# One bias column, one shared PSUM bank, VectorE's additions and three places in a schedule: a four-layer image kernel on one core

## The chip, the cores and the metric

The kernel runs on one core of a Trainium2 chip. Its time is device microseconds from the first to the last instruction, the median of several runs. The core has five engines that run beside each other: TensorE (PE, matmuls, with weight loads as PEld), VectorE (DVE), ScalarE (ACT), GpSimd (POOL) and SyncE (SP, which issues DMAs). Matmul results land in PSUM, in banks of 2 KB per partition; everything else lives in SBUF. Each engine executes its instructions in the order in which the program lists them, and waits on semaphores for the others.

## What is computed

The input x has 4 samples of 256 channels and 48 x 48 = 2304 positions, all in float32. Four layers follow, each of the form x = x + f(groupnorm(x)):

```python
def _gn(v, G=32, eps=1e-5):              # normalise over groups of 8 channels
    g = v.reshape(B_, G, C_ // G, H_, W_)
    m = jnp.mean(g, axis=(2, 3, 4), keepdims=True)
    s = jnp.var(g, axis=(2, 3, 4), keepdims=True)
    return ((g - m) / jnp.sqrt(s + eps)).reshape(v.shape)

# layer 0: attention with 8 heads of 64 channels over 2304 positions
qkv = jnp.einsum('oc,bchw->bohw', w_qkv, x)
q, k = _l2norm_last(q), _l2norm_last(k)          # over the positions
sim = jnp.einsum('bhdi,bhdj->bhij', q, k) * 10.0
out = jnp.einsum('bhij,bhdj->bhid', jax.nn.softmax(sim, axis=-1), v)
y0 = jnp.einsum('oc,bchw->bohw', w_out, out) + b_out

# layer 1: a gate from a depthwise convolution on a 16 x 16 grid
x_tem = _blur_pool(_max_pool_3x3(x), stride=3)   # 48 x 48 -> 16 x 16
s = x_h1 + x_w1 + x_h2 + x_w2                    # four depthwise strips of 11 x 3 taps
y1 = x * upsample(sigmoid(batchnorm(s)))

# layer 2: attention with one head of 64 channels, then a projection and a batch norm
f = jnp.einsum('bnc,bcm->bnm', theta_x, phi_x) * c1 ** (-0.5)
y2 = batchnorm(W @ (softmax(f) @ g_x))

# layer 3: a channel gate, a 3 x 3 depthwise convolution, an instance norm
y3 = leaky_relu(instancenorm(dwconv3x3(x * a)))
```

## The kernel before

The attentions are cut into blocks of 384 query positions (a "unit"). A unit takes its 2304 key positions in 18 blocks of 128, two to a group, so nine groups (NG = 9). For every group, TensorE makes the scores of this group and weighs the values of the last one; between the two it does what other jobs are placed in that group. ScalarE turns scores into exponentials (`pt`), eight buffers of which exist. The sums of the exponentials are added up in `acc` outside TensorE:

```python
PAIRED = (1, 3, 5, 7)

def scores(u, j):
    ps = sc_tile()                     # 2 buffers of 2 banks
    ...  # 4 matmuls, each on a quadrant of the array
    pt = ppool.tile([P, 2, SL], F32, tag="pt", name="pt")
    nc.scalar.activation(pt, ps[:, :, :SL], AF.Exp, scale=u["scale"])      # L277

def add_up(u, g):
    pts = [u["pt"][j] for j in range(g * G, (g + 1) * G)]
    terms = u.setdefault("terms", [])
    if g in u["paired"]:               # GpSimd adds the two blocks first
        half = hpool.tile([P, 2, SL], F32, tag="half", name="half")
        nc.gpsimd.tensor_add(half, pts[0], pts[1])                         # L302
        pts = [half]
        ready, u["terms"] = terms, pts
    else:
        ready, u["terms"] = terms + pts, []
    ...
    for term in ready:
        nc.vector.tensor_add(u["acc"], u["acc"], term)                     # L317
```

The main loop gives each group its order, and ScalarE's part of layer 1 (a product of a 16 x 16 image and one tap's weight, 761 ns each) in portions by the place of the group in its unit:

```python
QUOTA = (2, 1, 0, 1, 2, 1, 2, 1, 2)    # taps after group 0, 1, ... of a unit
AT_TOTAL, AT_FOLD, AT_INVERT, AT_DIVIDE, AT_AFTER = 3, 2, 5, 9, 11

for t, (u, g, st) in enumerate(groups):
    for j in range(g * G, (g + 1) * G):
        scores(u, j)
    do(fills, t, lambda rank: rank < 1)
    if prev is not None:
        add_up(*prev)
    do(due, t)
    ...
    do(fills, t)                       # jobs on TensorE, in the order of their rank
    ...                                # jobs of layer 1
    if prev is not None:
        ...  # weigh(pu, j) for the two blocks of the last group
        if pg == NG - 1:
            last(pu, t)                # ScalarE copies the result out of PSUM (raw)
    take_taps(QUOTA[clock["slot"]])
```

Beside one pair of heads, the projections of the next pair are made, one chunk of 384 columns per unit, in the unit's third group. All of these jobs, the output projection and the products of the group norms share two PSUM buffers, the `pj` tiles of one bank each:

```python
def pj_tile():
    return ps_pj.tile([P, 512], F32, tag="pj", name="pj")   # 2 buffers

# inside gn(): sums over the 8 channels of a group, by a product with gmat
def squares():
    ps = pj_tile()
    nc.tensor.matmul(ps[:, 0:NK], lhsT=gmat, rhs=mv[:, :, 0], start=True, stop=True)   # L197
    nc.vector.tensor_copy(gm, ps[:, 0:NK])
    ...
def inverse():
    ps = pj_tile()
    nc.tensor.matmul(ps[:, 0:NK], lhsT=gmat, rhs=res["sq"], start=True, stop=True)     # L207
    ...
# "placed" norms: both as jobs of rank 3.5 in a unit's third group, one unit apart

def out_bias():                        # one per pair of heads, in the third group of its second unit
    ps = pj_tile()
    for k in range(NK):
        nc.tensor.matmul(ps[:, k : k + 1], lhsT=wo[:, p, k * P : (k + 1) * P],
                         rhs=at["bias_v"], start=True, stop=True)                      # L550
    ...  # VectorE copies it to pair["bo"]

# a chunk: rank 1 q, rank 2 values, rank 3 k (each: products into a pj tile, ScalarE copies out)
# out_proj part(k): rank 2.5 (0 for sample 0) and rank 4
def part(k):
    ps = pj_tile()
    nc.tensor.matmul(ps[:, :SL], lhsT=wo[:, p, k * P : (k + 1) * P], rhs=o["o"], ...)  # L649
    nc.vector.scalar_tensor_tensor(                                                    # L654
        xs, ps[:, :SL], pair["bo"][:, k : k + 1], xs, ALU.add, ALU.add)
```

In layer 2 the projections of the next sample (L1009, L1030) have fixed places among the 27 groups of a sample, and so have the statistics of the output, which VectorE takes from PSUM (L1057, L1065):

```python
AT_PLACE = 6
if b > 0:
    spread(work, stats(b - 1, 1), [4, 5])
    spread(work, stats(b - 1, 2), [13, 14])
if b + 1 < B:
    spread(work, stats(b, 0), [22, 23])
    ...
    if b + 2 < B:
        for c in range(L2C):
            work[NG * c + AT_PLACE] = slices[c] + slices[c + L2C]
else:
    spread(work, stats(b, 0), [14, 15])
    spread(work, stats(b, 1), [23, 24])
```

Layer 0 of samples 1 to 3 runs beside layer 1 of the sample before it; layer 1 of the last sample runs beside layer 2.

Of the kernel before, what the change touches and what calls it, by code (L numbers as in the profile page):

```python
# [14 lines left out]
P = 128  # L15
HW = 48
N = HW * HW
NK = 2
# [56 lines left out]
def usual_path(  # L75
# [96 lines left out]


    GN_TICKS = NSL + 4

    def gn(b, res, halves=range(NK), slices=range(NSL), first=False, placed=False):

        if "st" not in res:
            res["st"] = small.tile([P, NK, NSL, 6], F32, tag="gn_st", name="gn_st")
        st = res["st"]  # L180
        if first:
            for s in slices:
                for k in halves:
                    nc.vector.bn_stats(st[:, k, s, :], X[b][:, k, s * SL : (s + 1) * SL])
        for s in () if first else slices:
            for k in halves:
                nc.vector.bn_stats(st[:, k, s, :], X[b][:, k, s * SL : (s + 1) * SL])
            if s % 2 or len(halves) == NK:
                yield 0
        mv = small.tile([P, NK, 2], F32, tag="gn_mv", name="gn_mv")  # L190
        for k in range(NK):
            nc.vector.bn_aggr(mv[:, k, :], st[:, k].rearrange("p s f -> p (s f)"))
        gm = small.tile([P, NK], F32, tag="gn_gm", name="gn_gm")

        def squares():
            ps = pj_tile()
            nc.tensor.matmul(ps[:, 0:NK], lhsT=gmat, rhs=mv[:, :, 0], start=True, stop=True)  # L197
            nc.vector.tensor_copy(gm, ps[:, 0:NK])
            dev = small.tile([P, NK], F32, tag="gn_dev", name="gn_dev")
            nc.vector.tensor_sub(dev, mv[:, :, 0], gm)  # L200
            res["sq"] = sq = small.tile([P, NK], F32, tag="gn_sq", name="gn_sq")
            nc.vector.tensor_mul(sq, dev, dev)
            nc.vector.tensor_add(sq, sq, mv[:, :, 1])

        def inverse():
            ps = pj_tile()
            nc.tensor.matmul(ps[:, 0:NK], lhsT=gmat, rhs=res["sq"], start=True, stop=True)  # L207
            gv = small.tile([P, NK], F32, tag="gn_gv", name="gn_gv")
            nc.vector.tensor_scalar(gv, ps[:, 0:NK], GN_EPS, None, ALU.add)
            res["rs_"] = small.tile([P, NK], F32, tag="gn_rs", name="gn_rs", bufs=6)  # L210
            rsqrt(res["rs_"], gv)

        def done():
            rs = res["rs_"]
            nm = small.tile([P, NK], F32, tag="gn_nm", name="gn_nm", bufs=6)
            nc.vector.tensor_scalar(nm, gm, -1.0, None, ALU.mult)
            nb = small.tile([P, NK], F32, tag="gn_nb", name="gn_nb", bufs=6)
            nc.vector.tensor_mul(nb, nm, rs)
            res["rs"], res["nb"], res["nm"] = rs, nb, nm

        if placed:

            t = clock["t"] + 1
            t += (AT_AFTER - t) % NG
            fills.setdefault(t, []).append((3.5, squares))
            fills.setdefault(t + NG, []).append((3.5, inverse))
            due.setdefault(t + NG + 3, []).append(done)
            yield 1
            return
        yield 3  # L230
        squares()
        yield 2
        inverse()
        yield 2
        done()
        yield 1
# [82 lines left out]
    def total(u):  # L319

        ab = [pj_tile()[:, :SL] for _ in range(2)]
        for h, c in enumerate(HALVES):
            for r, out in zip(HALVES, ab):
                nc.tensor.matmul(
                    out[c], lhsT=ones[r], rhs=u["acc"][r, h, :], start=True, stop=True
                )
        if "shift" in u["of"]:
            rows = [op.tile([P, SL], F32, tag="o", name="row") for _ in ab]
        else:
            row = hpool.tile([P, 2, SL], F32, tag="half", name="row")  # L330
            rows = [row[:, i, :] for i in range(2)]
        for i in range(2):
            nc.scalar.copy(rows[i], ab[i])
        u["l6"] = small.tile([P, 2, LW], F32, tag="l6", name="l6")
        for c in HALVES:
            for i in range(2):
                nc.sync.dma_start(
                    u["l6"][c, i, :],
                    rows[i][c.start : c.start + 1, :].rearrange("o (p w) -> o p w", w=LW),
                )  # L340
# [49 lines left out]
        nc.vector.tensor_add(lsum[:, 0:1], lsum[:, 0:1], two[:, 0:1])  # L390
        nc.vector.tensor_tensor(lmin[:, 0:1], lmin[:, 0:1], two[:, 1:2], ALU.min)

    due, fills, clock = {}, {}, {}

    taps_due = []

    QUOTA = (2, 1, 0, 1, 2, 1, 2, 1, 2)

    def take_taps(n):
        for _, fn in taps_due[:n]:  # L400
# [98 lines left out]
    def project(b, norm, pair):  # L499
# [18 lines left out]
        def norms():  # L518

            w = at["w"]  # L520
            ps = pj_tile()
            for k in range(NK):
                nc.tensor.matmul(
                    ps[:, 0:1], lhsT=w[:, k, 2, :], rhs=norm["nb"][:, k : k + 1],
                    start=k == 0, stop=k == NK - 1,
                )
            at["bias_v"] = small.tile([P, 1], F32, tag="bias_v", name="bias_v", bufs=3)
            nc.vector.tensor_copy(at["bias_v"], ps[:, 0:1])
            for k in range(NK):
                nc.scalar.activation(  # L530
                    w[:, k], w[:, k], AF.Identity, scale=norm["rs"][:, k : k + 1]
                )
# [11 lines left out]
                fetch(0)  # L544
                fetch(1)

        def out_bias():
            ps = pj_tile()
            for k in range(NK):
                nc.tensor.matmul(  # L550
                    ps[:, k : k + 1], lhsT=wo[:, p, k * P : (k + 1) * P],
                    rhs=at["bias_v"], start=True, stop=True,
                )
            bo = small.tile([P, NK], F32, tag="bo", name="bo", bufs=3)
            if p == 0:
                nc.vector.tensor_add(bo, ps[:, 0:NK], vec[:, V_BOUT, :])
            else:
                nc.vector.tensor_copy(bo, ps[:, 0:NK])
            pair["bo"] = bo

        def qk(s, t):
            cols = slice(s * SL, (s + 1) * SL)
            to = pair["qk"[t]][:, cols]
            n = SL + (s == 0 and not direct)
            ps = pj_tile()
            for k in range(NK):
                nc.tensor.matmul(  # L567
                    ps[:, :n], lhsT=at["w"][:, k, t, :], rhs=xs[s][:, k, :n],
                    start=k == 0, stop=k == NK - 1,
                )  # L570
            if s == 0 and direct:
                for k in range(NK):
                    nc.tensor.matmul(
                        ps[:, SL : SL + 1], lhsT=at["w"][:, k, t, :],
                        rhs=norm["nm"][:, k : k + 1], start=k == 0, stop=k == NK - 1,
                    )
            if s == 0:
                nc.scalar.copy(at["bias"][:, t : t + 1], ps[:, SL : SL + 1])
            if direct and t:

                nc.vector.tensor_scalar(to, ps[:, :SL], at["bias"][:, t : t + 1], None, ALU.add)
            else:
                nc.scalar.activation(to, ps[:, :SL], AF.Identity, bias=at["bias"][:, t : t + 1])
# [41 lines left out]
        def rescale(c0, c1):  # L625
# [7 lines left out]
            nc.vector.tensor_scalar(q, q, at["sc"], None, ALU.mult)  # L633

        return {
            "prefetch": prefetch, "norms": norms, "start": start, "out_bias": out_bias,
            "chunk": chunk, "qk": qk, "squares": squares, "values": values,
            "scale": [
                scale, lambda: rescale(0, 1), lambda: rescale(1, 3), lambda: rescale(3, 6)
# [3 lines left out]
    def out_proj(b, p, c, pair, o):  # L643
# [2 lines left out]

        def part(k):
            ps = pj_tile()
            nc.tensor.matmul(  # L649
                ps[:, :SL], lhsT=wo[:, p, k * P : (k + 1) * P], rhs=o["o"], start=True,  # L650
                stop=True,
            )
            xs = X[b][:, k, cols]
            nc.vector.scalar_tensor_tensor(  # L654
                xs, ps[:, :SL], pair["bo"][:, k : k + 1], xs, ALU.add, ALU.add
            )
# [3 lines left out]
    def l0_unit(b, p, c, pair):  # L660
        hold = {}

        def o_tile():
            hold["o"] = op.tile([P, SL], F32, tag="o", name="o")
            return hold["o"]

        return {
            "pt": {}, "qc": slice(c * SL, (c + 1) * SL), "paired": PAIRED,
            "soon": b == B - 1 and p == NPAIR - 1 and c == NCH - 1,
            "scale": 1.0, "of": pair, "o": o_tile,  # L670
            "after": out_proj(b, p, c, pair, hold),
# [182 lines left out]

    TAPS_AT_ONCE = 12

    AT_PLACE = 6

    def strips_pe(b, k, norm, res):

# [366 lines left out]
    for i, (b, p) in enumerate(order):  # L1227
        work, others = {}, []
        if i + 1 < len(order):
            new = projs[i + 1]  # L1230
            work[0] = [new["start"]]
            for s in range(NCH):
                work[NG * s + AT_CHUNK] = new["chunk"](s)
            work[NG + AT_CHUNK].append(new["out_bias"])
            for slot, fn in zip((n - 5, n - 3, n - 2, n - 1), new["scale"]):
                work[slot] = [fn]
            if i + 2 < len(order):
# [25 lines left out]
    for b in range(B):  # L1263
# [19 lines left out]
            if b + 2 == B:  # L1283
                others.append((follow(start, slices, norms2[b + 1]), 1000, 0, n))
        else:
            spread(work, stats(b, 0), [14, 15])
            spread(work, stats(b, 1), [23, 24])
            others.append((diagonals(), NK * len(PE_TAPS), 4, 22))
        phases.append(([l2_unit(b, c, twos[b]) for c in range(L2C)], work, others))
# [12 lines left out]
        fn()  # L1302
    for s in range(NCH):
        projs[0]["values"](s)
    projs[0]["out_bias"]()
    projs[1]["norms"]()
    attend(phases)
    for k in range(NK):
# [1278 lines left out]
```

## Time and profile before

| | |
|---|---|
| time, median of 3 runs | 3639.22 us (3636.34 to 3643.51) |
| span of the profiled run | 3637.4 us |
| mean granted TensorE clock | 0.985 |
| DMA | 95.69 MB, mean 26 GB/s |

In the profile, a line such as L649 is a line of the kernel. `pj<-o,wo` says that a tile `pj` is written from `o` and `wo`. A group of instructions has its count, the union of its busy times, the mean duration of one, and after the bar the idle time of its engine just before it, with what ended that idle time. An fp32 matmul leaves two records. In the table of waits, the columns are the total in us, the number of times and the longest.

### The profile page before, as it was taken

To read this page: it belongs to the slowest core of one execution; us is meant where nothing else is said; L and a number is where in the kernel's file an instruction comes from. 1 tells how busy PE (TensorE), PEld (TensorE's weight loads), DVE (VectorE), ACT (ScalarE), POOL (GpSimd) and SP (SyncE) were. 2 spreads that over 40 slices of the span, in tenths; PEclk is the share of its full clock that TensorE was granted. 3 is DMA by queue.
4 is the path that set the end of the run, shared out by engine and by line. 5 is a ranking of instruction groups with operands and counts; after the bars stand their busy time and mean duration, and the time that the engine had idled before them with its cause. 6 is when DMAs were issued, how large, how long until landed. Compare 5 with 4: busy or idle time off the path is not lost. (4 is left out here: it accounts for less than half of the span.)

```text
span 3637.4 us, 88927 instructions
## 1 busy us (share of the span) xinstructions
PE 3488.9 (96%) x37490; PEld 1762.7 (48%) x37490; DVE 2600.2 (71%) x3268; ACT 2423.3 (67%) x3889; POOL 1387.0 (38%) x886
## 2 busy tenths in 40 slices
PE   8999999999999999999999999999999998999786
PEld 4555555554444444544444445444444445654332
DVE  3555555577889787778797877777977778575678
ACT  4665666666875886668858866688588655554476
POOL 2333333333333333333333333333333356573333
PEclk9999999999999999999999999999999999999798
DMA  2211111111111111211111111111111100000001
GB/s 91 47 26 21 26 22 27 22 25 22 24 23 24 20 27 22 72 26 24 22 25 22 26 20 26 22 25 22 25 17 26 18 5 7 8 6 6 27 32 76
DMA packets 115433, 95.69 MB, mean 26 GB/s; under 512 B 56544, under 2 KB 110416, under 8 KB 114256
## 3 DMA queue, kind: packets, MB, share of 16 engines
q1 hardware_dynamic: 112128, 87.73, 13.2%
q8 instruction: 296, 4.85, 0.5%
q10 hardware_dynamic: 2896, 2.18, 0.2%
q14 instruction: 113, 0.93, 0.1%
HBM read 56.98 MB, written 11.80 MB: 19 GB/s over the span
## 5 line engine op out<-in xcount | busy, mean ns | idle before, releaser
L277 ACT ACTIVATE pt<-sc 128x768 f32<-128x768 f32 x1944 | 1475.5, 811 | 770.5 <-PE sc L271 762.0
L302 POOL TENSOR_TENSOR half<-pt 128x768 f32<-128x768 f32 x477 | 948.1, 1989 | 1604.0 <-ACT pt L277 1500.0
L271 PE MATMUL sc<-q,k 64*64 64x384 f32 x13824 | 1273.5, 483 | 5.1 <-ACT pt L277 5.1
L291 PE MATMUL av<-pt,v 64*64 64x384 f32 x13824 | 1276.8, 484 | 0.0
L317 DVE TENSOR_TENSOR acc<-acc,pt 128x768 f32<-128x768 f32 x792 | 958.7, 1210 | 80.9 <-DVE acc L317 1.8
L271 PEld LDWEIGHTS sc<-q,k 64*64 64x64 f32 x13824 | 521.5, 133 | 607.5 <-issue 536.5
L291 PEld LDWEIGHTS av<-pt,v 64*64 64x64 f32 x13824 | 519.1, 133 | 591.9 <-issue 559.3
L317 DVE TENSOR_TENSOR acc<-acc,half 128x768 f32<-128x768 f32 x459 | 476.6, 1038 | 300.9 <-POOL half L302 299.7
L654 DVE SCALAR_TENSOR_TENSOR x<-pj,bo,x 128x384 f32<-128x384 f32 x192 | 118.4, 617 | 438.6 <-PE pj L649 438.0
L827 ACT ACTIVATE prod<-pd,wt 128x256 f32<-128x256 f32 x486 | 336.1, 761 | 0.2
L567 PE MATMUL pj<-xs,w 128*128 128x384 f32 (+1 forms) x720 | 275.3, 505 | 1.7 <-POOL xs L511 0.9
L372 POOL TENSOR_TENSOR o<-o,rinv 128x384 f32<-128x384 f32 x95 | 117.0, 1232 | 362.9 <-DMA rinv<-rinv 330.9
L567 PEld LDWEIGHTS pj<-xs,w 128*128 128x128 f32 x720 | 124.1, 189 | 129.8 <-issue 35.9
L291 PE MATMUL av<-pt,qv 64*64 64x384 f32 x1728 | 178.3, 506 | 0.0
L649 PE MATMUL pj<-o,wo 128*128 128x384 f32 x384 | 161.9, 506 | 15.4 <-DVE x L654 8.1
L271 PE MATMUL sc<-qv,kd 64*64 64x384 f32 x1728 | 170.8, 489 | 2.4 <-ACT pt L277 2.4
L850 DVE TENSOR_REDUCE prod<-prod 128x256 f32<-128x1280 f32 x114 | 168.5, 1478 | 4.5 <-ACT prod L827 4.5
L311 DVE TENSOR_TENSOR acc<-pt 128x768 f32<-128x768 f32 x99 | 150.6, 1521 | 10.8 <-ACT pt L277 10.8
L1541 PE MATMUL one<-pad,diag 64*64 64x384 f32 x1536 | 136.6, 501 | 19.0 <-ACT pad L1511 11.8
L598 PEld LDWEIGHTS pj<-w,xs 128*128 128x128 f32 x1080 | 134.5, 191 | 24.1
L598 PE MATMUL pj<-w,xs 128*128 128x128 f32 x1080 | 134.9, 275 | 0.0
L368 POOL TENSOR_TENSOR o<-raw 128x384 f32<-128x384 f32 x95 | 117.6, 1238 | 0.0
(242 smaller groups left out, 2584.5 us busy)
## 6 DMA issues: line engine op xcount, KB each, us to landing
xs<-in_x_dram SPq DMA_DIRECT2D x90, 384.0 KB
rinv<-rinv SPq DMA_DIRECT2D x208, 94.5 KB
out_dram<-x SPq DMA_DIRECT2D x18, 384.0 KB
l<-row SPq DMA_DIRECT2D x416, 1.5 KB
w<-in_wqkv_dram SPq DMA_DIRECT2D x32, 192.0 KB
x<-in_x_dram SPq DMA_DIRECT2D x4, 1152.0 KB
x<-in_x_dram SPq DMA_DIRECT2D x9, 384.0 KB
rinv<-ls SPq DMA_DIRECT2D x208, 1.5 KB
```

What stands on the lines that cost most here:

```text
L271: nc.tensor.matmul(ps[c * D : (c + 1) * D, h, :SL], lhsT=u["of"]["k"][r, j0 : j0 + D], rhs=u["of"]["q"][r, u["qc"]], start=True, stop=True,)
L277: nc.scalar.activation(pt, ps[:, :, :SL], AF.Exp, scale=u["scale"])
L291: nc.tensor.matmul(u["av"][h * D : (h + 1) * D, half, :SL], lhsT=value(u, j, h)[r], rhs=pt[r, h, :], start=j == 0, stop=j == JB - 1,)
L302: nc.gpsimd.tensor_add(half, pts[0], pts[1])
L311: nc.vector.tensor_add(u["acc"], ready[0], ready[1])
L317: nc.vector.tensor_add(u["acc"], u["acc"], term)
L567: nc.tensor.matmul(ps[:, :n], lhsT=at["w"][:, k, t, :], rhs=xs[s][:, k, :n], start=k == 0, stop=k == NK - 1,)
L598: nc.tensor.matmul(ps[:, i * P : (i + 1) * P], lhsT=xs[s][:, k, i * P : (i + 1) * P], rhs=at["w"][:, k, 2, :], start=k == 0, stop=k == NK - 1,
L649: nc.tensor.matmul(ps[:, :SL], lhsT=wo[:, p, k * P : (k + 1) * P], rhs=o["o"], start=True, stop=True,)
L827: nc.scalar.activation(bufs[n % 3][:, :, min(n, 1) + i].rearrange("p (r c) -> p r c", c=AS), pd[:, PAD + dr : PAD + dr + AS, PAD + dc : PA ...
L850: nc.vector.tensor_reduce(to, bufs[n % 3][:, :, : min(n, 1) + len(taps)], AX.X, ALU.add)
L1541: nc.tensor.matmul(self.ps[s][h][HALVES[h ^ e], :SL].rearrange("p (r c) -> p r c", c=HW), lhsT=diag[self.k][r, 2 * n + e, :], rhs=self.win ...
```

## The change

It has five parts. The bias of the output projection no longer has matmuls of its own: it is written into a 385th column of the tile that the output projection multiplies anyway, once per pair of heads. The products of the group norms go into two unused columns of the PSUM bank that k's products have just been written to, so that they do not take a `pj` tile of their own. In layer 0 of samples 1 to 3, which runs beside layer 1, VectorE adds all 18 blocks itself, and GpSimd none. The portions of taps change for two places of a unit. In layer 2, the places of the projections are one group later, and two statistics steps of the last sample two groups later. The purpose is to take work and waits off TensorE.

```diff
+        def columns():
+            if of_k.get("t") == clock["t"]:
+                return of_k["ps"][:, 448 : 448 + NK]
+            return pj_tile()
+
         def squares():
-            ps = pj_tile()
+            ps = columns()
 ...
         def inverse():
-            ps = pj_tile()
+            ps = columns()
 ...
-    QUOTA = (2, 1, 0, 1, 2, 1, 2, 1, 2)
+    QUOTA = (1, 1, 0, 2, 2, 1, 2, 1, 2)
 ...
-        def out_bias():
-            ps = pj_tile()
-            for k in range(NK):
-                nc.tensor.matmul(
-                    ps[:, k : k + 1], lhsT=wo[:, p, k * P : (k + 1) * P],
-                    rhs=at["bias_v"], start=True, stop=True,
-                )
-            ...
 ...
             ps = pj_tile()                       # qk(s, t): t = 1 is k
+            if t:
+                of_k["ps"], of_k["t"] = ps, clock["t"]
 ...
         def part(k):
             ps = pj_tile()
+            n = SL + (c == 0)
             nc.tensor.matmul(
-                ps[:, :SL], lhsT=wo[:, p, k * P : (k + 1) * P], rhs=o["o"], start=True,
+                ps[:, :n], lhsT=wo[:, p, k * P : (k + 1) * P], rhs=o["o"][:, :n], start=True,
                 stop=True,
             )
+            if c == 0:
+                if k == 0:
+                    pair["bo"] = small.tile([P, NK], F32, tag="bo", name="bo", bufs=3)
+                bo = pair["bo"][:, k : k + 1]
+                if p == 0:
+                    nc.vector.tensor_add(bo, ps[:, SL:n], vec[:, V_BOUT, k : k + 1])
+                else:
+                    nc.vector.tensor_copy(bo, ps[:, SL:n])
 ...
         def o_tile():
-            hold["o"] = op.tile([P, SL], F32, tag="o", name="o")
-            return hold["o"]
+            hold["o"] = op.tile([P, SL + 1], F32, tag="o", name="o")
+            if c == 0:
+                nc.gpsimd.tensor_copy(hold["o"][:, SL:], pair["bias_v"])
+            return hold["o"][:, :SL]
 ...
-            "pt": {}, "qc": slice(c * SL, (c + 1) * SL), "paired": PAIRED,
+            "pt": {}, "qc": slice(c * SL, (c + 1) * SL), "paired": () if b else PAIRED,
 ...
-    AT_PLACE = 6
+    AT_PLACE = 7
 ...
-            work[NG + AT_CHUNK].append(new["out_bias"])
 ...
-            spread(work, stats(b, 0), [14, 15])
+            spread(work, stats(b, 0), [16, 17])
```

More of the change, by code (lines that the diff above doesn't have):

```diff
@@ L174, in usual_path @@
     GN_TICKS = NSL + 4
+    of_k, clock = {}, {"t": -1}
     def gn(b, res, halves=range(NK), slices=range(NSL), first=False, placed=False):
@@ L327, in total @@
         if "shift" in u["of"]:
-            rows = [op.tile([P, SL], F32, tag="o", name="row") for _ in ab]
+            rows = [op.tile([P, SL + 1], F32, tag="o", name="row")[:, :SL] for _ in ab]
         else:
@@ L391, in note @@
         nc.vector.tensor_tensor(lmin[:, 0:1], lmin[:, 0:1], two[:, 1:2], ALU.min)
-    due, fills, clock = {}, {}, {}
+    due, fills = {}, {}
     taps_due = []
-    QUOTA = (2, 1, 0, 1, 2, 1, 2, 1, 2)
+    QUOTA = (1, 1, 0, 2, 2, 1, 2, 1, 2)
     def take_taps(n):
@@ L526, in norms @@
                 )
-            at["bias_v"] = small.tile([P, 1], F32, tag="bias_v", name="bias_v", bufs=3)
-            nc.vector.tensor_copy(at["bias_v"], ps[:, 0:1])
+            pair["bias_v"] = small.tile([P, 1], F32, tag="bias_v", name="bias_v", bufs=3)
+            nc.vector.tensor_copy(pair["bias_v"], ps[:, 0:1])
             for k in range(NK):
@@ L545, in start @@
                 fetch(1)
-        def out_bias():
-            ps = pj_tile()
-            for k in range(NK):
-                nc.tensor.matmul(
-                    ps[:, k : k + 1], lhsT=wo[:, p, k * P : (k + 1) * P],
-                    rhs=at["bias_v"], start=True, stop=True,
-                )
[L554 to L559, printed above, removed]
         def qk(s, t):
@@ L635, in project @@
         return {
-            "prefetch": prefetch, "norms": norms, "start": start, "out_bias": out_bias,
+            "prefetch": prefetch, "norms": norms, "start": start,
             "chunk": chunk, "qk": qk, "squares": squares, "values": values,
@@ L1304, in usual_path @@
         projs[0]["values"](s)
-    projs[0]["out_bias"]()
     projs[1]["norms"]()
```

## The prediction

> **What bounds the kernel now.** I read the views in this order: busy time of the engines, stretches of the span, TensorE's waits, then the timeline around each kind of wait. First line 1 of the page:
>
> ```profile
> PE 3488.9 (96%) x37490; PEld 1762.7 (48%) x37490; DVE 2600.2 (71%) x3268; ACT 2423.3 (67%) x3889; POOL 1387.0 (38%) x886
> ```
>
> TensorE is busy 96% of the span. The table of stretches (us, then busy PE, PEld, DVE, ACT, POOL, granted clock, DMA) says where it is not:
>
> ```profile
> 750.00:2930.00 2180.00, 2153.06 (x23070) 1060.01 (x23066) 1709.68 (x1986) 1576.30 (x2535) 788.12 (x466) 1.00 0.15 25
> 2930.00:3445.00 515.00, 460.91 (x5070) 262.96 (x5066) 358.30 (x449) 264.56 (x416) 286.03 (x182) 0.93 0.07 10
> 40.00:750.00 710.00, 708.77 (x7678) 360.50 (x7680) 365.61 (x502) 431.85 (x688) 241.20 (x182) 1.00 0.15 29
> ```
>
> From 40 to 750 us (sample 0's attention) TensorE never rests. From 750 to 2930 (attention of samples 1 to 3 beside layer 1) 27 us are idle, in layer 2 (2930 to 3445) 54. So the only things that can move the time are instructions TensorE need not issue and waits that hold it. A page's busy time hides short waits, because a matmul's end is modelled. I therefore took start-to-start times: a block of eight quadrant matmuls (16 records) starts 1.29 us after the last when nothing holds it. By that measure TensorE loses about 4 us up to 750, 56 us from 750 to 2930 and about 60 in layer 2 and its end. Of the 56, some 22 (waits of about 0.1 us for evictions between q, v and k) are not touched by the change. The larger waits, from TensorE's table (total, times, longest):
>
> ```profile
> PE pj L649 <- DVE x L654: 8.1, 7, 1.8
> PE pj L1057 <- DVE bst L1065: 7.7, 5, 4.2
> PE sc L271 <- ACT pt L277: 7.5, 31, 2.4
> PE pj L1009 <- DVE bst L1065: 6.8, 3, 4.0
> PE pj L197 <- DVE x L654: 2.9, 3, 1.0
> PE pj L1030 <- DVE bias L984: 2.5, 1, 2.5
> ```
>
> Every one of them names an engine that is not full but late at one moment. The page's groups show why VectorE is late:
>
> ```profile
> L302 POOL TENSOR_TENSOR half<-pt 128x768 f32<-128x768 f32 x477 | 948.1, 1989 | 1604.0 <-ACT pt L277 1500.0
> L317 DVE TENSOR_TENSOR acc<-acc,pt 128x768 f32<-128x768 f32 x792 | 958.7, 1210 | 80.9 <-DVE acc L317 1.8
> ```
>
> The mean of 1210 ns mixes two kinds. Single records between 750 and 2930 take 958 ns where GpSimd is idle and up to 2.56 us where it runs.
>
> **What the Trainium skill says.** "SBUF — State Buffer", Who interferes with whom: a VectorE instruction with two SBUF inputs and a GpSimd instruction that reads SBUF exclude each other for a whole instruction. The trace agrees: 958 ns alone, 1.6 to 2.6 us beside a GpSimd add. Summing what VectorE's records last over the undisturbed duration of their own kind in 750 to 2930 gives 317 us, of which 269 overlap the pair adds of L302. "PSUM — Partial Sum Buffer", PSUM bank collisions: two engines must not touch one bank and quadrant at once, so a matmul into a bank that ScalarE is reading has to be held by a semaphore even if the columns differ. Nothing in the kernel before shows this; it decides part two below. "TensorE: Matmul & The Clock Gate", What's actually happening: idle TensorE is put on half clock for windows of about 3.4 us. The trace agrees: half-clock stretches of 3.4 or 6.8 us begin at 1164, 2772, 3089, 3236 and 3353 us, each right after a wait of 1.9 to 4.3 us. A long wait so costs half such a stretch more, 1.7 or 3.4 us.
>
> **Part 1, the bias column.** Four one-column matmul records (an fp32 matmul leaves two) leave each head pair, with their weight loads:
>
> ```profile
> 980.11 0.81 PE L649 MATMUL pj<-o,wo 128*128 128x384 f32 x2
> 980.95 0.61 PE L550 MATMUL pj<-bias_v,wo 128*128 128x1 f32 x4
> 981.48 1.52 PE L291 MATMUL av<-pt,v 64*64 64x384 f32 x16
> ```
>
> From the last projection to the next block are 1.37 us. Without the bias it would be 0.325 between the two passes + 0.415 to the next block = 0.74. So 0.63 us x 15 pairs = 9.4 us, all on TensorE's path. The 385th column costs 32 x 1/384 of 0.65 us, nothing. The bias takes 32 VectorE instructions of about 0.16 us in place of 16, and 16 more on GpSimd, all beside other work. Sum -9.
>
> **Part 2, the norms' products in k's bank.** Nine normalisations run inside the attention, two products each: 18. Here is one before (886.30 is k's product):
>
> ```profile
> 886.30 1.56 PE L567 MATMUL pj<-xs,w 128*128 128x384 f32 x4
> 887.69 0.28 PE L207 MATMUL pj<-gn_sq,gmat 128*128 128x2 f32 x2
> 887.89 0.58 ACT L583 ACTIVATE k<-pj,bias 128x384 f32<-128x384 f32 x1 [1.65 <-PE pj L567]
> 888.22 0.91 PE L649 MATMUL pj<-o,wo 128*128 128x384 f32 x2 [0.25 <-DVE gn_gv L209]
> ```
>
> Before, the product goes to the other bank and the projection after it waits 0.25 us for VectorE to read it. In the changed program the product carries a wait on ScalarE instead, that is on k's eviction, which ends at 888.47. It would then start near 888.52 rather than 887.69, and the projection near 888.85 rather than 888.22: 0.6 us later. Fifteen such, +9 us; the other three now wait 1.1 us for a late VectorE (line L197 of the waits) and would get 0.6 shorter, -2. Sum +7. This part should cost time.
>
> **Part 3, VectorE adds alone.** 72 blocks (samples 1 to 3, four pairs, six chunks). Per block before: one add at 1664 ns, eight at 1281, four at 993 = 15.9 us. After: 17 at about 0.958 = 16.3, plus what the two remaining GpSimd instructions per block (1.3 and 1.2 us) disturb. In sum 288 more adds x 0.958 = 276 us against 269 us of exclusion that goes: VectorE's busy time hardly changes. What changes is lateness: it no longer waits for `half` (106 us of idle time in that stretch) and no add lasts 2.5 us. At 1163 the projection waited 1.76 us behind two adds of 2.63, one of 2.56 and a maximum of 2.22 us. Without the pair add these come to about 2 us less. So most of the 8.4 us (start to start) behind L654, and the one wait at L984 (2.6 us, behind adds of 4.14 for two and 1.74), should go: -7 and -2. The half clock after the waits at 1163 and 2772 goes with them, 1.7 + 3.4 us: I count -4.
>
> **Part 4, the taps' quota.** Waits of `sc` on `pt` come once per block where taps run, 29 times, always in the group after a block's end, where ScalarE has the copy of `raw` and two taps. They show as 0.17 us, but start to start it is 1.64 instead of 1.29:
>
> ```profile
> 972.12 1.47 PE L291 MATMUL av<-pt,v 64*64 64x384 f32 x16
> 973.76 1.56 PE L271 MATMUL sc<-q,k 64*64 64x384 f32 x16 [0.17 <-ACT pt L277]
> ```
>
> One tap (0.5 us of ScalarE's issue) moves to the fourth group, where ScalarE idles 0.29 us before its next exponential. 29 x 0.345 = 10 us; I count -9.5.
>
> **Part 5, layer 2's places.** The three waits of L1009 (1.4, 4.1 and 1.5 us) come where the projections follow a statistics step of the group before; a group later VectorE has 2.6 us more: -5.5. At 3348.16 two statistics steps fall in one group and TensorE waits 4.3 us; in the change they are three groups apart: -4. Less half clock behind these, some 3 us. Sum -12.5.
>
> **Sum.** -9 + 7 - 13 - 9.5 - 12.5 = -37. Something unforeseen usually takes some of it back, so I take -33: 3606 us, 0.9% less.
>
> **Rivals.** (a) VectorE becomes the late engine. Per block of about 30 us beside the taps it has 16.3 us of adds, about 6 of reductions, 2 to 3 of the rest, and it must keep up group by group (1.92 of 2.58 us, and 1.48 more where a reduction falls). For it: the reductions sat in groups that had no add, and these have two now. Against: eight `pt` buffers and the long third group (7 us) absorb 2 to 3 us. If TensorE waited 0.5 us per block more, +36 us: 3640. (b) The bank of k: if ScalarE is later than in the sample shown, every norm's product costs 1 us, +9 more: 3615. (c) The waits removed are hidden behind others at once (the next group's `pj` waits for the same late VectorE). Then only parts 1 and 4 pay, against part 2: -12, about 3627. (d) Half clock: a stretch of 37.5 us at 3403 lies in the turn to layer 3, and costs up to 19 us; if the turn shifts it may shorten or lengthen, 5 to 10 us either way.
>
> **Range and chances.** (c) and (b) give the upper side, all parts in full with luck in the clock the lower: 3588 to 3630. Faster by over 2% would need 73 us, more than all named waits; slower by over 2% would need (a) twice over.
>
> **What would show it.** No L550 row; `sc <- ACT pt` down to a few; a new row of the norms' product waiting for ACT `k`, 18 times about 0.6 us idle; L302 at 189 instead of 477; L317 between 750 and 2930 at a mean near 1.0 us; `L649 <- x` and `L984` near zero; the rows with `bst` below 5 us together. I am wrong if VectorE's rows grow in TensorE's waits, or if the stretch from 750 to 2930 does not shrink by 15 us or more.

## The result and the profile after

The changed kernel takes 3605.97 us (median of 4 runs, 3603.77 to 3606.74) against 3639.8 us before (median of 4 runs, one more than in the table of the time before): ratio 0.9906, 95% interval 0.9889 to 0.9923, some 34 us less. In the changed kernel the lines have moved: L197 and L207 (the norms' products) are L204 and L214, L271 (scores) L278, L302 (pair adds) L309, L317 (adds) L324, L511 (a two-column copy on GpSimd that the projections read) L518, L649 and L654 (output projection and its addition) L645 and L658, L894 (layer 1's products) L901, L973 (a product for the bias of layer 2's projections) L980, L984 (that bias) L991, L1009 and L1030 (the projections) L1016 and L1037, L1057 and L1065 (statistics) L1064 and L1072.

The page's first part, and then the table of stretches over the same two windows as before:

```profile
PE 3469.3 (96%) x37426; PEld 1754.9 (49%) x37426; DVE 2607.0 (72%) x3572; ACT 2411.9 (67%) x3889; POOL 824.1 (23%) x614
```

```profile
750.00:2930.00 2180.00, 2163.09 (x23316) 1066.38 (x23310) 1746.58 (x2319) 1579.30 (x2556) 238.29 (x200) 1.00 0.15 25
2930.00:3445.00 515.00, 464.07 (x5150) 265.42 (x5146) 356.71 (x480) 274.48 (x439) 283.54 (x180) 0.94 0.06 10
```

TensorE's share is still 96%. In the first window its idle time fell from 27 to 17 us; in the second it hardly moved, from 54 to 51. GpSimd's busy time fell by 40%, and VectorE's busy time stayed at 2607 us, though it has 304 more instructions.

TensorE's waits (total, times, longest):

```profile
...
PE pj L901 <- DVE bst L1072: 6.7, 3, 4.1
...
PE pj L214 <- ACT k L578: 5.8, 8, 0.9
PE pj L204 <- ACT k L578: 5.4, 8, 0.7
...
PE pj L1064 <- DVE bst L1072: 5.1, 6, 1.0
...
PE sc L278 <- ACT pt L284: 2.9, 2, 2.4
...
PE pj L645 <- DVE x L658: 1.7, 4, 0.6
```

The rows for `pt`, for `x` and for layer 2's `bias` have gone or shrunk. The norms' products wait for ScalarE, as predicted. And a row that did not exist has come: L901, layer 1's products, waits three times for the statistics.

For the split by stage I take the time between two fixed points of the program: from the fifth to the sixteenth time that VectorE works out the scale of q. Between them lie eleven pairs of heads, the attention of samples 1 to 3 less its end. The same table over that stage and the rest, first before, then after:

```profile
747.30:2755.80 2008.50, 1988.02 (x21287) 978.68 (x21282) 1585.40 (x1841) 1458.63 (x2356) 731.47 (x432) 1.00 0.15 26
2755.80:3637.40 881.60, 770.93 (x8490) 408.94 (x8482) 638.29 (x899) 520.73 (x812) 413.49 (x261) 0.94 0.10 21
```

```profile
744.40:2725.40 1981.00, 1970.20 (x21232) 973.07 (x21228) 1590.08 (x2116) 1447.59 (x2356) 212.37 (x180) 1.00 0.15 26
2725.40:3602.00 876.60, 772.69 (x8502) 410.31 (x8494) 643.63 (x924) 520.45 (x813) 367.95 (x237) 0.94 0.10 21
```

The eleven pairs got 27.5 us shorter, the rest 5.0, and the start (to 744.4 in place of 747.3) 2.9. The 5.0 are more than accounted for by the end of sample 3's attention: the wait for `bias` (2.6 us start to start) and the half clock after it (6.8 us at half speed, so 3.4) are gone. So no gain of layer 2's new places shows here; how far the rest varies from run to run is said below.

### The profile page after: what moved, and what is told of

It reads as the page before. It is cut to its first block, busy times and chain, and to the rows that moved or that the text cites. A ratio compares the mean times of both kernels' runs of the same rounds, so it can differ in the third digit from the quotient of the medians.

```text
span 3602.0 us, 88972 instructions
## 1 busy us (share of the span) xinstructions
PE 3469.3 (96%) x37426; PEld 1754.9 (49%) x37426; DVE 2607.0 (72%) x3572; ACT 2411.9 (67%) x3889; POOL 824.1 (23%) x614
## 3 DMA queue, kind: packets, MB, share of 16 engines
q1 hardware_dynamic: 112128, 87.73, 13.3%
## 5 line engine op out<-in xcount | busy, mean ns | idle before, releaser
L324 DVE TENSOR_TENSOR acc<-acc,pt 128x768 f32<-128x768 f32 x1368 | 1367.8, 1000 | 176.4 <-ACT pt L284 76.7
L278 PE MATMUL sc<-q,k 64*64 64x384 f32 x13824 | 1269.9, 482 | 0.5 <-ACT pt L284 0.5
L278 PEld LDWEIGHTS sc<-q,k 64*64 64x64 f32 x13824 | 525.0, 133 | 590.4 <-issue 544.3
L309 POOL TENSOR_TENSOR half<-pt 128x768 f32<-128x768 f32 x189 | 363.4, 1926 | 551.8 <-ACT pt L284 520.0
L324 DVE TENSOR_TENSOR acc<-acc,half 128x768 f32<-128x768 f32 x171 | 190.4, 1114 | 235.2 <-POOL half L309 234.4
L658 DVE SCALAR_TENSOR_TENSOR x<-pj,bo,x 128x384 f32<-128x384 f32 x192 | 118.5, 617 | 316.2 <-PE pj L645 314.9
L278 PE MATMUL sc<-qv,kd 64*64 64x384 f32 x1728 | 172.4, 489 | 2.4 <-ACT pt L284 2.4
L645 PE MATMUL pj<-o,wo 128*128 128x384 f32 (+1 forms) x384 | 160.2, 501 | 5.8 <-issue 3.6
L375 POOL TENSOR_TENSOR o<-raw 128x384 f32<-128x384 f32 x95 | 125.8, 1324 | 51.9 <-ACT raw L371 51.5
L318 DVE TENSOR_TENSOR acc<-pt 128x768 f32<-128x768 f32 x99 | 114.7, 1159 | 25.8 <-ACT pt L284 25.8
```

What stands on the lines that cost most here:

```text
L278: nc.tensor.matmul(ps[c * D : (c + 1) * D, h, :SL], lhsT=u["of"]["k"][r, j0 : j0 + D], rhs=u["of"]["q"][r, u["qc"]], start=True, stop=True,)
L375: eng.tensor_add(u["sum"], u["raw"][:, 0, :], u["raw"][:, 1, :])
L645: nc.tensor.matmul(ps[:, :n], lhsT=wo[:, p, k * P : (k + 1) * P], rhs=o["o"][:, :n], start=True, stop=True,)
```

## The experiments

The theory: the predicted parts are right in their signs, and layer 2's places won little because their waits moved to L901. The rivals are named with each run. The five runs from "norms in a tile of their own" to "bias products back" each undo one part of the change, so a part's worth is how much longer the run is than the changed kernel. "Eleven pairs" is the stage above; "rest" is all after it. Both come from one profiled execution of each version.

| version | time, us | ratio to before, 95% interval | eleven pairs, us | rest, us |
|---|---|---|---|---|
| before | 3639.8 | 1 | 2008.5 | 881.6 |
| changed | 3605.97 | 0.9906 (0.9889 to 0.9923) | 1981.0 | 876.7 |
| changed, run again | 3602.18 | 0.9906 (0.9891 to 0.9921) | 1980.9 | 874.3 |
| norms in a tile of their own | 3594.93 | 0.9884 (0.9869 to 0.9899) | 1974.6 | 877.1 |
| pair adds back | 3620.48 | 0.9956 (0.9942 to 0.9969) | 1995.0 | 879.9 |
| quota back | 3617.12 | 0.9948 (0.9934 to 0.9961) | 1994.6 | 874.1 |
| places back | 3604.98 | 0.9915 (0.9902 to 0.9929) | 1980.9 | 879.2 |
| bias products back | 3614.72 | 0.9937 (0.9924 to 0.9951) | 1988.2 | 876.7 |
| norms after the projection | 3590.86 | 0.9872 (0.9856 to 0.9887) | 1971.7 | 875.1 |
| layer 1's products barred | 3588.61 | 0.9867 (0.9852 to 0.9882) | 1981.4 | 857.4 |
| statistics' place only | 3601.23 | 0.9900 (0.9885 to 0.9915) | 1980.9 | 873.2 |
| both mends | 3579.11 | 0.9836 (0.9823 to 0.9849) | 1971.7 | 858.2 |
| both, and k first | 3586.80 | 0.9864 (0.9849 to 0.9879) | 1982.7 | 856.4 |

The kernel before ran at 3636 to 3640 us beside these, so the ratio compares better across rows than the time. The stages repeat within 0.1 us for the eleven pairs and within 2.4 us for the rest (the two rows of the changed kernel). The second run of the changed kernel was expected within 3 us of 3606 and came out 3.8 us lower, at the same ratio.

**Norms' products in a tile of their own.**

```diff
         def columns():
-            if of_k.get("t") == clock["t"]:
-                return of_k["ps"][:, 448 : 448 + NK]
             return pj_tile()
```

> The changed kernel, but the norms' products take a pj tile of their own again, as before the change. Theory (the products in k's bank cost TensorE the wait for ScalarE's eviction of k, about 0.7 us idle in 14 of them, and nothing else is won by it): the waits of the norms' products for k vanish, and the time falls by 6 to 9 us to about 3598. Rival (with only two pj tiles, a tile less taken per norm saves at least as much, in waits for VectorE): the projection after the product waits 0.25 us for VectorE's read, some products wait 1 us for a late x, and the time stays within 2 us of 3606 or rises.

The eleven pairs took 6.4 us less, and the time was 3594.93 us, 11.0 less, or 8.0 by the ratios. The theory holds. The timeline of the changed kernel shows one such product (start, duration, engine, line; the idle time and its end in brackets):

```profile
882.07 1.56 PE L562 MATMUL pj<-xs,w 128*128 128x384 f32 x4
...
883.66 0.58 ACT L578 ACTIVATE k<-pj,bias 128x384 f32<-128x384 f32 x1 [1.65 <-PE pj L562]
...
884.30 0.38 PE L214 MATMUL pj<-gn_sq,gmat 128*128 128x2 f32 x2 [0.67 <-ACT k L578]
884.54 0.89 PE L645 MATMUL pj<-o,wo 128*128 128x384 f32 x2
```

k's eviction ends at 884.24, and the product starts 0.06 us later. From k's first product to the projection are 2.47 us, against 1.92 in the sample of the kernel before: 0.55 us lost. In the run with its own tile the row of `k` is gone and the old small waits (0.25 us, fourteen times) are back.

**Pair adds back on GpSimd.**

```diff
-            ... "paired": () if b else PAIRED,
+            ... "paired": PAIRED,
```

> The changed kernel, but GpSimd adds four pairs of blocks per unit in samples 1 to 3 again. Theory (the pair adds hold VectorE by excluding it from SBUF, so TensorE waits for x and for layer 2's bias): L302's count is 477 again, VectorE's adds average 1.2 us or more, the waits of the projections for x come back with 6 to 9 us between 750 and 2930, and the time rises by 8 to 13 us to about 3616. Rival (VectorE's busy time is the same either way, and the quota alone took the waits away): the time stays within 3 us of 3606.

The time was 3620.48 us; the eleven pairs took 14.0 us more and the rest 3.2. The whole time is 14.5 us over the changed kernel, where 8 to 13 were expected. The waits of this run between 745 and 2890 us:

```profile
PE pj L645 <- DVE x L658: 7.7, 10, 1.6
...
PE pj L562 <- POOL xs L518: 3.1, 5, 1.4
PE pj L1037 <- DVE bias L991: 2.5, 1, 2.5
```

The wait for `x` and the one for `bias` are back, and a third that the prediction had counted with nothing: TensorE waits 3.1 us for a two-column copy on GpSimd (L518) that stands behind a pair add. Start to start, the waits for `x` cost 8.1 us more in the eleven pairs than in the changed kernel and those for L518 3.5; 2.4 of the 14.0 I could not assign to a wait. VectorE's adds, in the changed kernel and then in this run, over the same stretch:

```profile
L324 DVE TENSOR_TENSOR acc<-acc,pt 128x768 f32<-128x768 f32 x1152 | 1143.9, 993 | 152.8 <-ACT pt L284 76.2 <-ACT row L340 0.9 <-DVE acc L324 0.9
```

```profile
L324 DVE TENSOR_TENSOR acc<-acc,pt 128x768 f32<-128x768 f32 x572 | 740.7, 1295 | 59.2 <-DVE acc L324 1.4 <-ACT row L340 0.5 <-ACT prod L834 0.5
L324 DVE TENSOR_TENSOR acc<-acc,half 128x768 f32<-128x768 f32 x286 | 281.9, 986 | 108.5 <-POOL half L309 108.5
```

A third more adds (1152 against 572 + 286), and those of `pt` 302 ns shorter in the mean: 1144 us against 740.7 + 281.9 = 1023. With its other work (a block's first maximum became shorter too) VectorE is busy equally long in the eleven pairs, 1590.08 us in the changed kernel and 1585.89 in this run:

```profile
744.30:2739.30 1995.00, 1974.20 (x21243) 974.21 (x21238) 1585.89 (x1852) 1454.28 (x2357) 748.22 (x443) 1.00 0.15 26
```

What counts is not the sum but the idle time before the adds. In this run 108.5 us of it end with `half`, in the changed kernel 76.2 with `pt`: VectorE waits for its next input instead of for GpSimd, so it is on time.

**The old portions of taps.**

```diff
-    QUOTA = (1, 1, 0, 2, 2, 1, 2, 1, 2)
+    QUOTA = (2, 1, 0, 1, 2, 1, 2, 1, 2)
```

> The changed kernel with the old portions of taps (2, 1, 0, 1, 2, 1, 2, 1, 2). Theory (the second tap after a unit's first group makes the exponentials late by 0.35 us once per unit with taps): some 29 waits of the scores for pt come back, 0.17 us each in the table of waits, and the time rises by 10 us to about 3616. Rival (the waits went because VectorE frees pt buffers sooner without GpSimd): the waits stay away, and the time stays within 2 us of 3606.

The time was 3617.12 us, and the eleven pairs took 13.6 us more. The waits of the scores came back, exactly 29 (this run, 745 to 2890 us):

```profile
PE sc L278 <- ACT pt L284: 6.1, 29, 0.2
```

Start to start they are 0.39 us each, 11.3 in all. The rival is out: with VectorE on time they still come. Some 2 us of the 13.6 I could not assign to a wait.

**Layer 2's old places.**

```diff
-    AT_PLACE = 7
+    AT_PLACE = 6
-            spread(work, stats(b, 0), [16, 17])
+            spread(work, stats(b, 0), [14, 15])
```

> The changed kernel with layer 2's old places (projections in the 7th group, the last sample's first statistics in groups 15 and 16). Theory (the three waits of the projections for the statistics only moved to the products of layer 1, which took the free group; what is won is the two statistics steps pulled apart): waits of L1009's successor for bst come back with 7 us, those of the layer 1 products fall by 7 us, one wait of 4 us for bst returns at the last sample, and the time rises by 2 to 5 us to about 3609. Rival (the places are worth the 12.5 us that the prediction gave them): the time rises by 10 us or more.

The ratio was 0.9915 against 0.9906, and the intervals overlap; the rest took 2.5 to 4.9 us more. The waits of this run:

```profile
PE pj L1064 <- DVE bst L1072: 8.8, 5, 4.0
PE pj L1016 <- DVE bst L1072: 6.5, 3, 3.9
```

Three waits of the projections (L1016) stand where the changed kernel has three of layer 1's products (L901), 6.5 against 6.7 us. One wait of 4.0 us at the last sample's statistics is back, and with it a half-clock stretch of 6.8 us.

**The bias' own products back.** The function `out_bias` and its place as in the kernel before; `n = SL` in the projection, and no bias column in `o`.

```diff
+            work[NG + AT_CHUNK].append(new["out_bias"])
...
-            n = SL + (c == 0)
+            n = SL
```

> The changed kernel with the bias' own products (one per pair, in the third group of its second unit) back, and no 385th column. Theory (each costs TensorE 0.63 us that nothing hides): the time rises by 9 us to about 3615, and the sum over the twelve pairs of samples 1 to 3 by 7 us. Rival (the products fill time in which TensorE waits for k's eviction anyway): less than 4 us.

The eleven pairs took 7.2 us more, the four of sample 0 another 2.8 (707.8 against 705.0). The time was 3614.72 us, 12.5 more than the changed kernel beside it, or 11 by the ratios. The products themselves:

```profile
L557 PE MATMUL pj<-bias_v,wo 128*128 128x1 f32 x64 | 9.5, 252 | 0.4
```

**Norms' products in k's bank, after the second projection.**

```diff
-            fills.setdefault(t, []).append((3.5, squares))
-            fills.setdefault(t + NG, []).append((3.5, inverse))
+            fills.setdefault(t, []).append((4.5, squares))
+            fills.setdefault(t + NG, []).append((4.5, inverse))
```

> The changed kernel with the norms' products still in k's bank, but after the second projection of the group rather than before it. Theory (their price is the wait for ScalarE to leave the bank, 0.8 us after k's last product, and the projection's 0.65 us cover it): the waits of the norms' products for k shrink from 0.7 to about 0.1 us each and the time falls by 8 us or more to about 3597, as it did with a tile of their own. Rival (a product into a bank that is being read costs more than the wait, or the order matters to VectorE): the time stays within 3 us of 3606.

3590.86 us, 11.3 less than the changed kernel beside it, and the eleven pairs 9.3 less. Between 745 and 2890 us two waits of the norms' products for k are left:

```profile
PE pj L214 <- ACT k L578: 0.4, 2, 0.2
```

So the bank as such costs nothing here; its price was a wait that another instruction can cover. This is 2.9 us better in the eleven pairs than a tile of its own, and the waits of the projections for VectorE's read of a norm's product (14 times 0.25 us there) are gone too.

**Layer 1's products barred from three groups.**

```diff
             taken.update(b * n + len(order) * NCH * NG + s for s in at)
+            taken.update(
+                b * n + len(order) * NCH * NG + NG * c + AT_PLACE - 1
+                for c in {0: (2,), 1: (0, 1)}.get(b, ())
+            )
```

> The changed kernel, with layer 1's products barred from the three groups of layer 2 in which they waited for the statistics (they come later instead). Theory (the waits of 1.3, 4.2 and 1.7 us belong to whatever takes the next pj tile; with an empty group VectorE has 2.6 us more): the rows of L901's successor for bst fall from 6.7 us to 2 us or less, one wait of 1.5 us may turn up at the projections after them, and the time falls by 4 to 7 us to about 3600. Rival (the wait moves again to the next user of a pj tile, or layer 1 ends later and holds layer 2's last sample): the time stays within 3 us of 3606 or rises.

3588.61 us, 13.6 less, where 4 to 7 were expected; the rest of the program took 857.4 us in place of 874 to 877. Its waits between 2880 and 3380 us:

```profile
PE pj L1064 <- DVE bst L1072: 7.4, 5, 4.1
...
PE pj L1016 <- DVE bst L1072: 2.5, 2, 1.6
...
PE pj L901 <- DVE bst L1072: 0.8, 1, 0.8
```

Of 7.2 us (start to start) at L901, 2.7 are left at L1016 and the 0.8 of the last line at L901. The table of the changed kernel also had a wait of 2.9 us for `acc`, one of 2.4 for `pt` and one of 3.2 at L980 in this stretch; with the products elsewhere none of them occurs. The row of L1064 grew by 2.3.

Up to about 3000 us the two programs give TensorE the same work in the same order. From there to layer 3's first product, the changed kernel, its second run and this run show:

```profile
3000.59:3387.10 386.51, 346.05 (x3917) 206.50 (x3909) 257.75 (x320) 198.70 (x317) 218.23 (x144) 0.96 0.08 12
```

```profile
2996.75:3385.70 388.95, 347.63 (x3917) 206.75 (x3909) 257.49 (x319) 198.52 (x317) 216.33 (x144) 0.95 0.08 12
```

```profile
2996.77:3369.90 373.13, 340.21 (x3917) 202.19 (x3909) 259.74 (x320) 198.76 (x317) 217.28 (x144) 0.96 0.08 12
```

This stretch is 13 to 16 us shorter. TensorE's idle time fell from 40.5 and 41.3 us to 32.9, and its busy time, on the same 3917 records, from 346 and 348 to 340: more than half of the gain is waits, the rest less busy time for the same work. TensorE was busy at half clock for 23.5 and 26.7 us of the stretch, and for 15.6 in this run; by my estimate, half of the difference, that is 4 to 6 us. That there is less of it because the waits are gone is argued, not shown. The half clock between the end of the eleven pairs and this stretch also differs (13.7 and 3.4 us against none), but there the two programs are the same, so that is no effect of the edit.

**Only the statistics' place.**

```diff
-    AT_PLACE = 7
+    AT_PLACE = 6
```

> The changed kernel with layer 2's projections in the 7th group again, and only the last sample's statistics left where the change put them (groups 17 and 18). Theory (the later place of the projections won nothing, since the layer 1 products took its waits over; the statistics' place won the 2 to 3 us between both old places and the change): the waits of L1009's successor for bst are back with 7 us, those of L901 are gone, and the time is within 3 us of the changed kernel. Rival (both halves matter and offset each other): the time differs by more than 5 us from the changed kernel.

Ratio 0.9900, within noise of 0.9906. The projections wait again, and L901 no longer does for `bst`:

```profile
PE pj L1016 <- DVE bst L1072: 6.5, 3, 3.9
```

The later place of the projections gained nothing: the rest is 873.2 us here against 876.7 and 874.3 with it. Against the run with neither new place (879.2) the rest is 6.0 us shorter, so what part five is worth seems to be the statistics' place: one wait of 4 us less and no half-clock stretch with it. By the whole times the two runs are not clearly apart (0.9885 to 0.9915 and 0.9902 to 0.9929).

**Both mends together.** The two diffs above.

> The changed kernel with the norms' products after the second projection and layer 1's products barred from the three groups after the statistics. Theory (the two lie in different stages and add up, 11 and 14 us): 25 us under the changed kernel, about 3578, ratio to the kernel before 0.984. Rival (what is won in the attention shifts layer 2 and its half clock, and part is lost): more than 6 us short of the sum, above 3584.

3579.11 us, ratio 0.9836 (0.9823 to 0.9849). From 0.9906 the two single gains, 0.0034 and 0.0039, would give 0.9833: they add up. The rest, 858.2 us against 875.1 with the norms' edit alone, shows the gain of the barred groups a second time. It is the fastest version here, 1.6% under the kernel before.

**And k before the first projection.**

```diff
-        return [((2.5 if b else 0, 4)[k], lambda k=k: part(k)) for k in range(NK)]
+        return [((3.2 if b else 0, 4)[k], lambda k=k: part(k)) for k in range(NK)]
```

> As the version with both, and besides in samples 1 to 3 the first output projection comes after k's products and not before them, so that k no longer takes the bank that ScalarE is just emptying of the values. Theory (128 slow starts of 0.1 us and 64 of 0.08 us in k's products, 18 us together, are that wait): these go, the second projection waits 0.2 us for k instead, and the time falls by 4 to 10 us, to about 3571. Rival (two projections in a row wait for k's eviction and for VectorE's read, and cost as much): within 3 us of the version with both.

A miss: 3586.80 us, slower than the version with both, and 11.0 us more in the eleven pairs. The group of the projections in this run:

```profile
L645 PE MATMUL pj<-o,wo 128*128 128x384 f32 (+1 forms) x384 | 164.4, 512 | 18.0 <-DVE x L658 10.0 <-issue 3.6 <-ACT k L578 1.8
```

The slow starts of k's products fell by half (13.3 to 6.6 us, start to start) and the wait for the values' eviction (5.5 us) went, but the second projection now stands right behind k and behind the first projection's addition. It waits 11.0 us for k and 12.2 for `x`, start to start. All 14 waits for `x` stand in the groups in which a norm's product follows into k's bank. The second pass of that projection also starts 0.1 us late (6.6 us in all); at the norms' products and around them about as much is saved.

## Why the prediction was right, and where it was not

The time was 3606.0 us, as predicted. That it was met this closely is luck: one large part was wrong, two others were worth more than was counted, and the 4 us that the prediction held back happened to cover what was left.

- **Part 1, bias, -9.** Right. The run without it shows 7.2 us in eleven pairs and 2.8 in four: 0.65 and 0.70 per pair against 0.63 worked out.
- **Part 2, norms in k's bank, +7.** Right in sign, cause and size: 6.4 us in the eleven pairs and, from the same run, 0.7 in sample 0 (705.0 against 704.3). The prediction counted 18 products behind k; there are 16, and each idles 0.70 us in the mean, not 0.6. The product was to start 0.83 us after its natural place; in the sample it starts 1.16 us after k's last product record in place of the usual 0.325. The rule of the Trainium skill, "PSUM — Partial Sum Buffer", PSUM bank collisions, that decided this sign is agreed with by the traces as far as they show the wait. No run here has the two accesses at once.
- **Part 3, VectorE alone, -13.** Right in mechanism, low by 4: 14.0 us in the eleven pairs and 3.2 after them. The term left out was GpSimd's own lateness, 3.1 us at L518 (3.5 start to start), of which the kernel before had shown 0.9. The half clock, counted with 4, was a single stretch of 3.4 us in the run with pair adds, behind the wait for `bias`: by the estimate of half its length, 1.7 us. The exclusion that the skill describes under "SBUF — State Buffer", Who interferes with whom, shows in an add's mean of 993 against 1295 ns.
- **Part 4, quota, -9.5.** Right in mechanism; with VectorE alone the term was 11.3 us, not 10, since each wait was 0.39 us rather than 0.345, and the stage lost 13.6, 2 of them unassigned.
- **Part 5, layer 2's places, -12.5.** Wrong. The step that failed is "a group later VectorE has 2.6 us more: -5.5". It is true of the projections, but it took L1009 for the only candidate for that group. The groups that the places leave free are at once used by layer 1's products, which take whichever group is not reserved, and they met the same late VectorE: waits of 1.3, 4.2 and 1.7 us in place of 1.4, 4.1 and 1.5. That is rival (c) of the prediction, in the stage where it was not looked for. Pulling the statistics apart turned one wait of 4.3 us into two of 0.8 and 1.2, and the half-clock stretch of 6.8 us that came with it went. The whole part is worth 3 us by the ratios and 2.5 to 4.9 by the rest, neither clear of noise.

Rival (a), VectorE as the late engine, did not come: its rows shrank, and it idles 76 us waiting for `pt`. Rival (b) was too dark: none of the norms' products idled over 0.9 us before its start. Rival (d), the half clock at the turn to layer 3, hardly moved: 37.5 us in one stretch before, 34.2 in two after. The prediction's reading of the half clock was too simple: of the ten stretches between 1100 and 3400 us in the kernel before, four (2953, 3045, 3137 and 3182 us) began with no wait over 1.2 us in the 3.4 us ahead of them, and waits of 1.56 us at 1893 and 1.94 at 3022 were followed by none. TensorE also need not be idle for a whole such stretch: the one at 1164 began after a wait of 1.76 us. So what a single wait costs in half clock can't be told from its length. Of what was to show the prediction, the count of the pair adds (189), the missing bias rows, the row for k and the mean of the adds (993 ns) came as stated, and the attention shrank by more than the 15 us asked for. "The rows with `bst` below 5 us together" did not: L901, L1064 and L980 hold 15 us (17.7 before). The parts as measured one by one, -10 + 7 - 17 - 14 - 3, give -37; together they gave -34. The 3 us between them are no more than the noise of the rest and of the single ratios.

## What to carry to other kernels

A wait belongs to a buffer, not to the instruction that the table names. Before moving that instruction, ask which instruction takes its place in the queue; if a free slot is filled by others, reserve it, or the wait only changes its name. Putting a product into a PSUM bank that is still being evicted cost the wait for the eviction here (0.70 us idle per product), so put it after work that covers it. And when GpSimd takes work off VectorE with operands in SBUF, compare VectorE's mean per instruction with and without it: here the help cost as much as it gave (1586 us busy with it, 1590 without).

## What was not expected

Barring layer 1's products from three groups, where they waited 7 us, gained 13.6 us. In the stretch that the edit changes, some 8 us of idle time went, with three waits that the theory had not named (for `acc`, for `pt` and at L980), and TensorE was also busy 6 to 7 us less on the same records, of which the half clock, by the estimate above, is 4 to 6. And moving one projection by a rank removed 12 us of slow starts and waits and made 23 us of new ones, so that this order of the users of two PSUM buffers is worse than the one it replaced.
